# Attention scores and weighted sums in quarters of the TensorE array instead of halves

## The chip, the cores and the metric

The kernel runs on one core of a Trainium2 chip. The metric is the device time of one execution in microseconds (us). Before the change the median of three runs is 1355.07 us (1351.96 to 1355.53).

## The reference

One transformer layer: cross attention with 16 heads, then a three-layer feed-forward network with sign weights, both with a residual. Everything is float32. The change lies in the attention, so only that is shown:

```python
# x: (1, 2048, 256)   context: (1, 1601, 192)   16 heads of 64
x = layer_norm(x, g_norm)
q = x @ Wq                                   # 256 -> 1024
k, v = split(context @ Wkv)                  # 192 -> 2 x 1024
k = concatenate([null_k, k]); v = concatenate([null_v, v])    # 1602 keys per head
sim = einsum('bhid,bhjd->bhij', q * s, k * s)                 # s = 64 ** -0.25
sim = where(mask, sim, -big)
attn = softmax(sim)
out = einsum('bhij,bhjd->bhid', attn, v)
out = layer_norm(out.reshape(b, -1, 1024) @ Wout, g_out)
```

## The kernel before

**Units.** Two heads form a pair, and each head of a pair takes 64 partitions of the tensors that have the head dimension on partitions. There are 8 pairs (`NP`) and 4 blocks of 512 queries (`NB`), so 32 units (p, b), worked through in this order. The 1602 keys (`KEYS`) lie in 13 tiles (`KC`) of 128; the last has 66 (`KLAST`).

**A unit's score stage.** For each key tile k, `exps` issues the scores of both heads, keys on partitions and 512 queries along the free axis, into one of two PSUM tiles `sT` (L296). Each head is one float32 matmul with 64 rows of contraction and 128 columns of weights: the first head uses rows 0 to 63 of the array, the second rows 64 to 127, each writes its own PSUM bank. Keys are stored as differences: `keys_stepped` (GpSimd, L221) subtracts from each key tile the one two tiles back, so that the scores accumulate in the two PSUM tiles from k to k + 2. For k of 0 and 1 two more matmuls (L307, float32r, 64 × 128) add the negative row maximum. ScalarE then reads the tile, adds the mask as a bias per key and writes the exponentials `e` (L309). GpSimd adds the `e` of all key tiles into `acc` (L498, L500), from which the softmax denominator is made later.

Between the scores of one key tile and of the next, the unit issues work for the next unit's row maxima: `max_chunk`, two float32r matmuls of 64 rows by 128 columns over 400 keys (L259), one for each head, which VectorE reduces (L262). There are 16 of these chunks over 13 key tiles, two of them after key tiles 0, 4 and 8.

**A unit's sums stage.** `weighted` goes over the 13 key tiles once more and accumulates the weighted sums of values into `av` (L316): for each head one float32 matmul with 128 rows (keys) and 64 columns; the first head's result goes to partitions 0 to 63, the second's to 64 to 127, of the same PSUM bank. After the third key tile `divided` is called for the unit before: two float32 matmuls of 128 rows by 64 columns (L334) give the denominators, and VectorE takes the reciprocal and multiplies with `avs`. At the end ScalarE copies `av` from PSUM to `avs` (L542).

**Between the stages.** TensorE does projections for the next pair of heads (`project_k`, L207; `project_v`, L230), the output projection of the unit before (`project_out`, L324), a small transpose (L272) and the query projection (`project_q`, L196), all on the whole array.

**Order.** All of this is written out by hand in `tc.manual_schedule()`: instructions stand on each engine's queue in the order of the code. PSUM is split in two pools of two tiles of two banks each: `spare` (scores, `av`, output projection and some others) and `flex` (maxima, denominators and some others). Each further tile of a pool waits until its predecessor in the same buffer has been read.

Each float32 matmul shows as two matmuls, each with its weight load, in the trace; a float32r matmul shows as one.

Of the kernel before, what the change touches and what calls it, by code (L numbers as in the profile page):

```python
# [9 lines left out]
F32 = mybir.dt.float32  # L10
F32R = mybir.dt.float32r
U8 = mybir.dt.uint8
AF = mybir.ActivationFunctionType
ALU = mybir.AluOpType
# [6 lines left out]
KEYS = M + 1  # L21
CD = 192
HEADS, DH = 16, 64
# [3 lines left out]
NB = N // 512  # L27
KC = (KEYS + 127) // 128
KLAST = KEYS - 128 * (KC - 1)
CHUNKS = ((0, 402), (402, 400), (802, 400), (1202, 400))  # L30
EPS = 1e-5
MASKED = -3.0e38
# [3 lines left out]
def xattn_ffn(ctx, tc, x, ctxT, mask, g_norm, null_kv, wq, wkv, wout, g_out, k0, k1, k2, s0, s1, s2, out):  # L36
    nc = tc.nc
# [11 lines left out]
    def spare(name):  # L49
        return ps_s.tile([128, 2, 512], F32, tag="s", name=name)  # L50
# [92 lines left out]
    with ExitStack() as att:  # L143
        ap = att.enter_context(tc.tile_pool(name="att", bufs=1))
        pp = att.enter_context(tc.tile_pool(name="pair", bufs=2))
# [10 lines left out]
        maskb = ap.tile([128, KC], F32, name="maskb")  # L156
        ones_r = ap.tile([128, 128], F32R, name="ones_r")
# [23 lines left out]
        pairs, queries = {}, {}  # L181

        def open_pair(p):
            pairs[p] = (
                pp.tile([128, KEYS], F32, tag="kT", name=f"kT_{p}"),
                pp.tile([128, KC, 128], F32, tag="v", name=f"v_{p}"),
                pp.tile([128, KEYS], F32R, tag="kr", name=f"kr_{p}"),
            )

        def project_q(p, b, get=flex):  # L190

            qT = wp.tile([128, 512], F32, tag="qT", name=f"qT_{p}_{b}")
            qr = wp.tile([128, 512], F32R, tag="qr", name=f"qr_{p}_{b}", bufs=1)
            ps = get(f"psq_{p}_{b}")
            for c in range(2):
                nc.tensor.matmul(ps[:, 0, :], weights[p][0][:, c, :], xnT[:, b, c, :], start=c == 0, stop=c == 1)  # L196
            nc.scalar.mul(qr, ps[:, 0, :], DH**-0.5)  # L197
            nc.scalar.mul(qT, ps[:, 0, :], DH**-0.5)
            queries[p, b] = (qT, qr)

        def project_k(p, n, get=flex):
            kT, _, kr = pairs[p]
            start, w = CHUNKS[n]
            keys = ds(start, w)
# [11 lines left out]
        def keys_stepped(p):  # L216

            kT = pairs[p][0]
            for at in range(256 * ((KEYS - 1) // 256), 0, -256):
                w = min(256, KEYS - at)  # L220
                nc.gpsimd.tensor_tensor(kT[:, ds(at, w)], kT[:, ds(at, w)], kT[:, ds(at - 256, w)], ALU.subtract)  # L221

        def project_v(p, n, get=flex):
            v = pairs[p][1]
            tiles = range(4 * n, min(4 * n + 4, KC))
            rows = 128 if n < 3 else KLAST
            ps = get(f"psv_{p}_{n}")
# [23 lines left out]
        def max_chunk(p, b, n, get=flex):  # L251
            t, c = divmod(n, 4)
            if n == 0:
                maxima[p, b] = wp.tile([128, 4, 2, 4], F32, tag="mx", name=f"mx_{p}_{b}")
            start, w = CHUNKS[c]
            ps = get(f"max_{p}_{b}_{n}")
            for j in range(2):
                rows = ts(j, DH)
                nc.tensor.matmul(  # L259
                    ps[:, j, :w], queries[p, b][1][rows, ts(t, 128)], pairs[p][2][rows, ds(start, w)], start=True, stop=True  # L260
                )
            nc.vector.tensor_reduce(maxima[p, b][:, t, :, c], ps[:, :, :w], AX.X, ALU.max)  # L262
# [15 lines left out]
                ALU.mult,  # L278
            )

        def rows_of(k):
            return 128 if k < KC - 1 else KLAST

        def exps(p, b, k, sT):

            kT, qT, mT = pairs[p][0], queries[p, b][0], shifts[p, b]
            n = rows_of(k)
            ps = sT[k % 2]
            for j in range(2):
                rows = ts(j, DH)
                nc.tensor.matmul(  # L296
                    ps[:n, j, :],
                    kT[rows, ds(128 * k, n)],
                    qT[rows, :],
                    start=k < 2,  # L300
                    stop=k >= 2,
                    skip_group_check=k >= 2,
                )
            if k < 2:
                for j in range(2):
                    rows = ts(j, DH)
                    nc.tensor.matmul(ps[:n, j, :], ones_r[rows, :n], mT[rows, :], start=False, stop=True)  # L307
            e = ep.tile([128, 2, 512], F32, tag="e", name=f"e_{p}_{b}_{k}")
            nc.scalar.activation(e[:n], ps[:n], AF.Exp, bias=maskb[:n, k : k + 1])  # L309
            return e  # L310

        def weighted(p, k, e, av):
            v = pairs[p][1]
            n = rows_of(k)
            for j in range(2):
                nc.tensor.matmul(  # L316
                    av[ts(j, DH), 0, :], v[:n, k, ts(j, DH)], e[:n, j, :], start=k == 0, stop=k == KC - 1
                )

        def project_out(p, b, aoT):  # L320
# [55 lines left out]
        def load_x(b):  # L376
            nc.sync.dma_start(out=x_sb[:, ts(b, 4), :], in_=x[ts(b, 512), :].rearrange("(c p) d -> p c d", p=128))

        load_pair(0)
        for b in range(1, NB):  # L380
            load_x(b)
        for n, (at, w) in enumerate(CHUNKS):
            skip = 1 if n == 0 else 0
# [11 lines left out]
        for j in range(2):  # L395
# [6 lines left out]
        nc.gpsimd.dma_start(  # L402
            out=mcol_u8[:KLAST, KC - 1 : KC], in_=mask[ds(128 * (KC - 1) - 1, KLAST)].rearrange("(p o) -> p o", o=1)
        )
# [5 lines left out]
        for j, s in enumerate((s0, s1, s2)):  # L410
            nc.gpsimd.dma_start(out=s_sb[:, j : j + 1], in_=s.partition_broadcast(128))
        nc.gpsimd.memset(mcol, 0.0)
        nc.gpsimd.memset(maskb, 0.0)
        nc.gpsimd.memset(ones, 1.0)
        nc.gpsimd.memset(fan, 1.0)

        nc.scalar.activation(warm, eps_sb, AF.Sqrt)

        open_pair(0)
        xn = input_root(0)  # L420
        nc.vector.tensor_scalar(ones_r, ident, 0.0, 1.0, ALU.mult, ALU.add)
# [10 lines left out]
        for t in range(4):  # L432
            max_chunk(0, 0, 4 * t + 1, slot)
            if t == 1:
                project_k(0, 3, slot)
                keys_stepped(0)
# [6 lines left out]
        nc.vector.tensor_scalar(  # L443
            maskb[:KLAST, KC - 1 : KC], mcol_u8[:KLAST, KC - 1 : KC], -MASKED, MASKED, ALU.mult, ALU.add
        )
# [16 lines left out]
        with tc.manual_schedule():  # L462
            for u, (p, b) in enumerate(units):
                nxt = units[u + 1] if u + 1 < len(units) else None
                if b == 0 and p + 1 < NP:
                    load_pair(p + 1)
                    open_pair(p + 1)
# [16 lines left out]
                es, n = [], 0  # L484
                acc = lp.tile([128, 2, 512], F32, tag="acc", name=f"acc_{p}_{b}")
                for k in range(KC):
                    if k == 0:

                        odd = spare(f"sT_{p}_{b}_1")
                        sT = [spare(f"sT_{p}_{b}_0"), odd]  # L490
                    es.append(exps(p, b, k, sT))
                    for _ in range(2 if k in extra else 1):
                        if nxt is not None:
                            max_chunk(*nxt, n)
                            n += 1
                    m = rows_of(k)
                    if k == 1:
                        nc.gpsimd.tensor_tensor(acc, es[0], es[1], ALU.add)  # L498
                    elif k > 1:
                        nc.gpsimd.tensor_tensor(acc[:m], acc[:m], es[k][:m], ALU.add)  # L500
                if nxt is not None:
                    max_combined(*nxt)
                else:
# [13 lines left out]
                av = spare(f"av_{p}_{b}")  # L517
                for k in range(KC):
                    weighted(p, k, es[k], av)
                    if k == 2 and last is not None:  # L520
                        aoT = divided(*last, flex(f"den_{p}_{b}")[:, 0, :])
# [18 lines left out]
                    nc.vector.tensor_tensor(s_out, s_out, s_sb[:, 2:3], ALU.mult)  # L540
                avs = lp.tile([128, 512], F32, tag="avs", name=f"avs_{p}_{b}", bufs=1)
                nc.scalar.copy(avs, av[:, 0, :])  # L542

                if u < 2:
                    input_turned(u + 2)
                if p + 1 < NP:
                    for n in ahead[b][0]:
                        project_v(p + 1, n, spare if n % 2 else flex)
                    for n in ahead[b][1]:
                        project_k(p + 1, n, spare if n % 2 else flex)  # L550
                    if b == 2:
                        keys_stepped(p + 1)
# [143 lines left out]
```

## Time and profile before

| | |
|---|---|
| median of three runs | 1355.07 us |
| the profiled execution | 1355.55 us |
| its span, first to last instruction | 1353.7 us |
| granted TensorE clock | 0.992 |
| busy: TensorE, VectorE, ScalarE, GpSimd | 1329.3, 880.7, 607.7, 994.8 us |
| before the first unit's scores | 51.4 us |
| a unit's score stage | 16.5 us (the last unit 16.7) |
| a unit's sums stage | 12.2 us |
| between the stages | 3.7 to 8.6 us |
| the feed-forward network at the end | 191.6 us |

The stages are read from the timeline of TensorE: a score stage goes from the first matmul of L296 to the first of L316, a sums stage from there to the end of the last of L316. TensorE's matmuls overlap in the records, [...]so what one piece of work takes is read from end to end, not from its own recorded length.

### The profile page before, as it was taken

Reading aid. Unit: us, or ns where it says so; the run is one execution under the profiler, and the core shown is the slowest. Engines: PE = TensorE matmul, PEld = TensorE weight load, DVE = VectorE, ACT = ScalarE, POOL = GpSimd, SP = SyncE. Lnnn points to the kernel's source line nnn. Section 1 sums busy time; section 2 is a strip of 40 time slices with the busy share of each in tenths; the row PEclk is TensorE's granted clock in tenths of the full one; section 3 lists DMA queues with packets and bytes.
Section 4 is the critical chain, followed back from the end, with each engine's and each line's share of the span. In section 5 each row is a group of like instructions: output and inputs, shape, how many; then the busy total and the mean of one; then the engine's idle time right before and its main releaser. Section 6 shows DMA issues by size and latency. Waiting matters only on the chain.

```text
span 1353.7 us, 16255 instructions
## 1 busy us (share of the span) xinstructions
PE 1329.3 (98%) x6528; PEld 664.6 (49%) x6528; DVE 880.7 (65%) x957; ACT 607.7 (45%) x655; POOL 994.8 (73%) x492
## 2 busy tenths in 40 slices
PE   6999999999999999999999999999999999999998
PEld 3544444444444444444444444444444443688887
DVE  5677776676667756686767656767676884464431
ACT  1666454445444454444544454454445557421220
POOL 4377987798888987798779877987798999711100
PEclk9799999999999999999999999999999999999999
DMA  5000000000000000000000000000000010000000
GB/s 136 4 1 7 0 1 8 8 1 0 8 1 7 1 1 8 7 1 1 7 8 1 1 8 8 0 1 5 0 16 1 1 39 0 1 0 16 16 16 16
DMA packets 14940, 12.31 MB, mean 9 GB/s; under 512 B 2240, under 2 KB 14784, under 8 KB 14864
## 3 DMA queue, kind: packets, MB, share of 16 engines
q1 hardware_dynamic: 13552, 9.70, 2.5%
q10 hardware_dynamic: 832, 1.23, 0.3%
q8 instruction: 51, 0.84, 0.3%
q0 software_dynamic: 480, 0.34, 0.1%
q14 instruction: 25, 0.20, 0.1%
HBM read 9.17 MB, written 2.10 MB: 8 GB/s over the span
## 4 chain that ended last, share of the span: by engine, by line
PE 93%; DVE 3%; ACT 2%; DMA 1%; issue 0%; POOL 0%; SPq 0%; ACTq 0%
PE sT L296 28%; PE av L316 27%; PE ps L592 10%; PE max L259 8%; PE psq L196 4%; PE po L324 4%; PE psv L230 3%; PE psk L207 3%; PE ps L615 2%; PE den L334 2%; ACT e L309 1%; PE sT L307 1%; DVE mx L262 1%; DMA x_sb<-in_x 1%; PE xT L361 0%
## 5 line engine op out<-in xcount | busy, mean ns | idle before, releaser
L500 POOL TENSOR_TENSOR acc<-acc,e 128x1024 f32<-128x1024 f32 (+1 forms) x352 | 847.3, 2407 | 27.6
L262 DVE TENSOR_REDUCE mx<-max 128x2 f32<-128x800 f32 (+1 forms) x512 | 481.3, 988 | 70.9 <-PE max L259 61.2
L309 ACT ACTIVATE e<-sT,maskb 128x1024 f32<-128x1024 f32 (+1 forms) x416 | 460.0, 1115 | 64.0 <-PE sT L296 38.0
L296 PE MATMUL sT<-qT,kT 64*128 64x512 f32 (+1 forms) x1664 | 444.4, 612 | 1.6 <-ACT e L309 1.4
L316 PE MATMUL av<-e,v 128*64 128x512 f32 (+1 forms) x1664 | 369.5, 594 | 1.0
L259 PE MATMUL max<-kr,qr 64*128 64x400 f32 (+1 forms) x1024 | 285.7, 568 | 2.3 <-DVE mx L262 1.5
L316 PEld LDWEIGHTS av<-e,v 128*64 128x64 f32 (+1 forms) x1664 | 116.7, 137 | 239.0 <-issue 219.3
L259 PEld LDWEIGHTS max<-kr,qr 64*128 64x128 f32 x1024 | 97.3, 186 | 187.2 <-DVE mx L262 149.7
L296 PEld LDWEIGHTS sT<-qT,kT 64*128 64x128 f32 (+1 forms) x1664 | 135.3, 181 | 104.8 <-ACT e L309 81.5
L498 POOL TENSOR_TENSOR acc<-e,e 128x1024 f32<-128x1024 f32 x32 | 75.5, 2358 | 147.6 <-ACT e L309 147.6
L542 ACT COPY avs<-av 128x512 f32<-128x512 f32 x32 | 18.8, 587 | 327.0 <-PE av L316 327.0
L336 DVE RECIPROCAL aoT<-den 128x512 f32<-128x512 f32 x31 | 104.1, 3357 | 70.0 <-PE den L334 70.0
L197 ACT ACTIVATE qr<-psq 128x512 fp32r<-128x512 f32 x32 | 19.1, 597 | 139.1 <-PE psq L196 139.1
L592 PE MATMUL ps<-h0hi,w 128*128 128x512 f32 x256 | 79.5, 392 | 0.0
L592 PE MATMUL ps<-h0lo,w 128*128 128x512 f32 x256 | 78.9, 389 | 0.0
L211 DVE TENSOR_TENSOR kT<-psk,keep 128x400 f32<-128x400 f32 (+1 forms) x32 | 18.4, 574 | 90.0 <-PE psk L207 89.8
L119 POOL TENSOR_TENSOR y_sb<-y_sb,gout_sb 128x256 f32<-128x256 f32 x12 | 9.3, 776 | 90.1 <-DVE y_sb L86 90.1
L581 DVE SCALAR_TENSOR_TENSOR h1lo<-ps,h1hi 128x1024 fp32r<-128x1024 f32 x16 | 19.6, 1224 | 69.0 <-ACT h1hi L580 69.0
L196 PE MATMUL psq<-xnT,wq 128*128 128x512 f32 x128 | 62.2, 610 | 0.6 <-DVE kT L211 0.6
L324 PE MATMUL po<-wo,aoT 128*128 128x256 f32 x256 | 61.5, 383 | 0.0
L329 DVE TENSOR_TENSOR y_sb<-po,y_sb 128x1024 f32<-128x1024 f32 x28 | 34.2, 1220 | 40.0 <-PE po L324 39.8
L580 ACT ACTIVATE h1hi<-ps 128x1024 fp32r<-128x1024 f32 x16 | 16.4, 1027 | 94.6 <-PE ps L592 94.6
(125 smaller groups left out, 1054.8 us busy)
## 6 DMA issues: line engine op xcount, KB each, us to landing
x_sb<-in_x SPq DMA_DIRECT2D x4, 512.0 KB, 8.7
out_x<-o SPq DMA_DIRECT2D x8, 256.0 KB, 2.1
wkv<-in_wkv SPq DMA_DIRECT2D x16, 96.0 KB, 2.1
wq<-in_wq SPq DMA_DIRECT2D x8, 128.0 KB, 2.3
wo<-in_wout SPq DMA_DIRECT2D x8, 128.0 KB, 2.1
xnT<-in_k SPq DMA_DIRECT2D x1, 1024.0 KB, 5.9
ctx_sb<-in_ctxT ACTq DMA_DIRECT2D x3, 300.0 KB, 7.9
xnT<-in_k SPq DMA_DIRECT2D x1, 512.0 KB, 3.9
```

Of the source, the lines that this page charges most:

```text
L196: nc.tensor.matmul(ps[:, 0, :], weights[p][0][:, c, :], xnT[:, b, c, :], start=c == 0, stop=c == 1)
L207: nc.tensor.matmul(ps[:, 0, :w], weights[p][1][:, c, 0, :], ctx_sb[:, c, keys], start=c == 0, stop=c == 1)
L259: nc.tensor.matmul(ps[:, j, :w], queries[p, b][1][rows, ts(t, 128)], pairs[p][2][rows, ds(start, w)], start=True, stop=True)
L262: nc.vector.tensor_reduce(maxima[p, b][:, t, :, c], ps[:, :, :w], AX.X, ALU.max)
L296: nc.tensor.matmul(ps[:n, j, :], kT[rows, ds(128 * k, n)], qT[rows, :], start=k < 2, stop=k >= 2, skip_group_check=k >= 2,)
L309: nc.scalar.activation(e[:n], ps[:n], AF.Exp, bias=maskb[:n, k : k + 1])
L316: nc.tensor.matmul(av[ts(j, DH), 0, :], v[:n, k, ts(j, DH)], e[:n, j, :], start=k == 0, stop=k == KC - 1)
L324: nc.tensor.matmul(pv[:, t, :], aoT[:, ts(t, 128)], weights[p][2], start=True, stop=True)
L336: nc.vector.reciprocal(aoT, ps)
L498: nc.gpsimd.tensor_tensor(acc, es[0], es[1], ALU.add)
L500: nc.gpsimd.tensor_tensor(acc[:m], acc[:m], es[k][:m], ALU.add)
L592: nc.tensor.matmul(ps[:, f, :], w(c)[:, ts(2 * g + f, 128)], parts[part][:, c, :], start=i == 0, stop=i == len(steps) - 1,)
```

## The change

Scores: each head's matmul of 64 rows by 128 columns becomes two of 64 × 64, one for each half of the key tile, so that four matmuls per key tile use the four quarters of the array. Weighted sums: each head's matmul of 128 rows by 64 columns becomes two of 64 × 64, one for each half of the keys; the two key halves accumulate in two PSUM banks, and after the ScalarE copy of the first bank VectorE adds the second to it. The last key tile is filled up to 128 keys: the key and value tiles are cleared there by GpSimd, the mask bias is set so that the exponentials are zero, and every operation on it works on 128 rows. The maxima, the shift matmuls of L307 and the denominators stay as they were.

```diff
+KP = 128 * KC
...
         def open_pair(p):
             pairs[p] = (
-                pp.tile([128, KEYS], F32, tag="kT", name=f"kT_{p}"),
+                pp.tile([128, KP], F32, tag="kT", name=f"kT_{p}"),
                 pp.tile([128, KC, 128], F32, tag="v", name=f"v_{p}"),
                 pp.tile([128, KEYS], F32R, tag="kr", name=f"kr_{p}"),
             )
+            nc.gpsimd.memset(pairs[p][0][:, KEYS:], 0.0)
+            nc.gpsimd.memset(pairs[p][1][DH:, KC - 1, :], 0.0)
...
         def keys_stepped(p):
-            for at in range(256 * ((KEYS - 1) // 256), 0, -256):
-                w = min(256, KEYS - at)
+            for at in range(256 * ((KP - 1) // 256), 0, -256):
+                w = min(256, KP - at)
...
+        QUARTERS = ((0, 0), (0, 1), (1, 0), (1, 1))
...
-            for j in range(2):
+            for j, c in QUARTERS:
                 rows = ts(j, DH)
                 nc.tensor.matmul(
-                    ps[:n, j, :],
-                    kT[rows, ds(128 * k, n)],
+                    ps[ts(c, 64), j, :],
+                    kT[rows, ds(128 * k + 64 * c, 64)],
                     qT[rows, :],
...
-            nc.scalar.activation(e[:n], ps[:n], AF.Exp, bias=maskb[:n, k : k + 1])
+            nc.scalar.activation(e, ps, AF.Exp, bias=maskb[:, k : k + 1])
...
         def weighted(p, k, e, av):
-            for j in range(2):
+            for r, j in QUARTERS:
+                rows = ts(r, 64)
                 nc.tensor.matmul(
-                    av[ts(j, DH), 0, :], v[:n, k, ts(j, DH)], e[:n, j, :], start=k == 0, stop=k == KC - 1
+                    av[ts(j, DH), r, :], v[rows, k, ts(j, DH)], e[rows, j, :], start=k == 0, stop=k == KC - 1
                 )
...
-        nc.gpsimd.memset(maskb, 0.0)
+        nc.gpsimd.memset(maskb, MASKED)
...
-                        nc.gpsimd.tensor_tensor(acc[:m], acc[:m], es[k][:m], ALU.add)
+                        nc.gpsimd.tensor_tensor(acc, acc, es[k], ALU.add)
...
                 nc.scalar.copy(avs, av[:, 0, :])
+                nc.vector.tensor_tensor(avs, av[:, 1, :], avs, ALU.add)
```

## The prediction

> **What bounds the kernel now.** I read the page's busy times first, then its chain that ended last, then its costliest groups.
>
> ```profile
> PE 1329.3 (98%) x6528; PEld 664.6 (49%) x6528; DVE 880.7 (65%) x957; ACT 607.7 (45%) x655; POOL 994.8 (73%) x492
> ...
> PE 93%; DVE 3%; ACT 2%; DMA 1%; issue 0%; POOL 0%; SPq 0%; ACTq 0%
> PE sT L296 28%; PE av L316 27%; PE ps L592 10%; PE max L259 8%; PE psq L196 4%; PE po L324 4%; PE psv L230 3%; PE psk L207 3%; PE ps L615 2%; PE den L334 2%; ACT e L309 1%; PE sT L307 1%; DVE mx L262 1%; DMA x_sb<-in_x 1%; PE xT L361 0%
> ...
> L262 DVE TENSOR_REDUCE mx<-max 128x2 f32<-128x800 f32 (+1 forms) x512 | 481.3, 988 | 70.9 <-PE max L259 61.2
> L309 ACT ACTIVATE e<-sT,maskb 128x1024 f32<-128x1024 f32 (+1 forms) x416 | 460.0, 1115 | 64.0 <-PE sT L296 38.0
> ```
>
> TensorE owns the chain, and the two edited lines, L296 (scores) and L316 (weighted sums), are 55% of it. Since a busy TensorE is not TensorE at its peak, the next view is the timeline of its matmuls, around one passage into a score stage and one into the sums. Columns: start, length (us), line, tile, shape, count.
>
> ```profile
> 404.36 1.88 PE L196 MATMUL psq<-xnT,wq 128*128 128x512 f32 x4
> 406.17 1.13 PE L296 MATMUL sT<-qT,kT 64*128 64x512 f32 x4
> ...
> 408.85 0.41 PE L259 MATMUL max<-kr,qr 64*128 64x400 f32 x2
> 409.10 1.02 PE L296 MATMUL sT<-qT,kT 64*128 64x512 f32 x4
> ...
> 410.29 1.13 PE L296 MATMUL sT<-qT,kT 64*128 64x512 f32 x4
> 410.85 0.75 PE L259 MATMUL max<-kr,qr 64*128 64x402 f32 x2
> ...
> 421.88 0.75 PE L259 MATMUL max<-kr,qr 64*128 64x400 f32 x2
> 422.68 2.80 PE L316 MATMUL av<-e,v 128*64 128x512 f32 x12
> 425.30 1.03 PE L334 MATMUL den<-acc,ones 128*64 128x512 f32 x4
> 426.16 8.76 PE L316 MATMUL av<-e,v 128*64 128x512 f32 x40
> ```
>
> Ends are compared, as starts overlap. (1) One key tile of sums is two float32 matmuls, which run as four. The last 40 end 8.59 us after the four of the denominator (434.92 − 426.33): 0.215 us each, 0.86 us per key tile. (2) A key tile of scores costs the same: the four at 409.10 end 0.86 us after the maxima ahead of them (410.12 − 409.26). (3) A pair of maxima adds 0.18 us to the scores ahead of it (411.60 − 411.42).
>
> So a score stage needs 13 × 0.86 + 16 × 0.175 + 2 × 0.23 (the L307 pairs, by the same reading) = 14.4 us of TensorE. It lasts 16.5 us:
>
> ```profile
> 406.17:422.68 16.51, 16.47 (x90) 7.20 (x89) 14.17 (x17) 14.48 (x15) 11.97 (x6) 1.00 0.05 14
> 422.68:434.92 12.24, 12.24 (x57) 4.00 (x57) 7.40 (x4) 0.99 (x1) 11.93 (x5) 1.00 0.00 1
> ```
>
> (Window, length, then busy time of PE, PEld, DVE, ACT, POOL, with counts.) VectorE's 16 reductions at 0.988 us are 15.8 us and start 1.6 us into the stage, so VectorE sets its length, ScalarE is close (13 × 1.115 = 14.5 us) and TensorE has about 2 us of slack. The sums stage is TensorE alone: 13 × 0.86 + 0.86 + 0.2 = 12.2 us.
>
> **What the Trainium skill says.** "TensorEngine Tiling (Array Packing)", section Key Properties: changing the tiling mode, not just the tile, drains TensorE. The trace agrees and gives the price. From projection (whole array) to scores (two row halves) the four matmuls end 1.06 us after their predecessors (407.30 − 406.24) instead of 0.86: 0.20 us. From row-half maxima to column-half sums the first twelve take 2.85 us (425.48 − 422.63) against 12 × 0.215 = 2.58: 0.27 us, part of it perhaps a wait for the exponential. Between scores and maxima, both on row halves today, the price is nil by (2). The same page, section Restrictions and Gotchas, says different row tiles must write different banks; the edit's two banks obey that. "TensorE: Matmul & The Clock Gate", section The mechanism, has matmuls in strict program order. The trace disagrees: each float32 matmul runs twice in a row on its own tile, yet the four at 406.17 take 0.86 us of streaming and not the 1.29 that strict order would give, so matmuls of different tiles do pass each other. That matters for four tiles.
>
> **The change, part by part.**
>
> *Quartering, array work.* Two halves already fill the 128 × 128 array. Quarters make 8 runs per key tile where 4 were, each over the same 512 columns, four at a time instead of two: 2 rounds of 0.43 us before and after. Gain 0. The sums stage before already has two streams out of the same partitions, and the scores before already write two banks of the same partitions, so neither should slow the quarters. Issue: 16 weight loads and matmuls per 0.86 us are 54 ns each; twenty such pairs of L230, over 128 columns, take 2.49 us in the timeline from 398.85 on, about 0.2 us of it the first load and the last end, so 115 ns a pair where quarters need 107. At worst that is 8 × 8 = 64 ns per key tile, 27 us over the sums stages; in the score stages the switches leave issue time to catch up. I take 0.
>
> *Alternation, the cost.* Scores become 64 × 64 tiles while the maxima (L259) and shift matmuls (L307) stay 64 × 128 and are still issued after every key tile. So each key tile switches the mode twice. Per unit: 13 switches out of scores, 12 back in. Entry into the stage and exit to the sums switch mode already. At 0.195 us: 25 × 0.195 = 4.9 us. TensorE needs 14.4 + 4.9 = 19.3 us. That passes VectorE's 15.8 and ScalarE's 14.5, so the slack of 2 us is eaten first and TensorE sets the stage. With 0.2 us for entry and exit it is 19.5 us instead of 16.5: +3.0 us. What is queued behind a switch is everything, since TensorE issues in order; its readers (exp, reductions) merely idle. A score waits for the exponential two tiles back: 2 us apart in the new rhythm against 1.115 us plus handover, so no new wait there. 31 units have maxima: 31 × 3.0 = **+93 us**. The last has none: 4 switches in its first two key tiles, +0.4 us at most 0.8.
>
> *Denominator inside the sums.* L334 stays on 128 × 64 tiles amid quarters: two switches, 0.39 us, in 31 units: **+12 us**.
>
> *Added vector sum.* `avs` = bank 1 + `avs`, 128 × 512 from PSUM; nearest rows are L274 (0.68 us) and L211 (0.57 us). It starts after the ScalarE copy (0.59 us), about 1.4 us after the last sum. The space between stages hides it: there TensorE runs projections for 3.7 to 8.6 us and VectorE idles 3.8 us before its first eviction. The next but one PSUM tile of that pool is not asked for sooner than about 1.8 us after the sums. If the cover failed it would cost up to 0.7 us × 32 = 22 us. I take 0.
>
> *Padding and clearing.* 16 GpSimd clears of 62 and 128 columns (a 128 × 128 clear took 0.23 us), the last step of `keys_stepped` 128 wide instead of 66 (between 0.33 and 0.73 us), additions of 128 rows instead of 66 (2.41 against 2.40 us), full exponentials instead of 66 rows (1.115 against 1.111). GpSimd's 13 steps a unit, about 31 us, fit the shortest unit of 32.5 us and gain room as units lengthen. SP's loads are not moved. Cost 0.
>
> **Sum.** 93 + 12 + 0.4 = 105. The profiled execution took 1355.55 us (span 1353.7), half a microsecond above the median of 1355.07. So 1355.5 + 105 = **1460 us**.
>
> **Rivals.**
> - *Four streams don't run at once, only two.* Then every key tile costs 0.86 us more in both stages: 26 × 0.86 × 32 = +715 us, about 2175 us. For: no 64 × 64 tile appears in the trace. Against: the passing of matmuls shown above. 8%.
> - *The switch is free between quarters and row halves.* Then the score stage stays VectorE's at 16.5 us and only the denominator may cost: 1356 to 1368 us. Against: every change of tile shape that the trace has costs 0.2 us or more. 5%, three of it slower.
> - *Faster: a quarter's round is shorter than 0.43 us.* The place is the 52 rounds a unit in both stages. At a round of 0.43 − x the added 3.4 us per unit are paid back when 52x > 3.4, at x = 65 ns. At x = 115 ns the score stage is back at VectorE's limit and the sums are 2.6 us shorter, about 1355 − 32 × 2.6 = 1272 us. For: smaller weight loads (137 against 186 ns). Against: those are hidden already, as 0.43 us per round is the same at both load lengths. 5%.
> - That the quarters aren't issued as written can't be: the instruction order has four score matmuls per key tile.
>
> **Numbers.** The likeliest case has 82%. Its range comes from the price of a switch between 0.14 and 0.27 us (stage 18.2 to 21.4 us; 53 to 153 us, the denominator 9 to 17), plus at most 27 us for issue: 1410 to 1540 us. That leaves the other cases out. The smallest difference to be told from no change is about 0.3%, 4 us. Slower 92% (82 + 8, and part of the free switch), same 3%, faster 5%.
>
> **What would show it.** Right: a score stage of about 19.5 us with scores' and maxima's ends spread by 0.2 us at each alternation; VectorE and ScalarE waiting in it for TensorE; sums stage 12.6 us; about 1.44 us per key tile. Wrong: a key tile of sums at 1.7 us (no four streams) or clearly under 0.86 us; a score stage still at 16.5 us; TensorE waiting for the added vector sum.

## The result, and the profile after

The changed kernel takes 1448.21 us (median of four runs, 1445.68 to 1448.76) against 1353.71 us before, measured beside it: 1.0694 times as long, 95% interval 1.0672 to 1.0716. The forecast was 1460 us in 1410 to 1540. The profiled execution took 1448.76 us, its span is 1447.0 us, 93.3 us more than before.

The page of the changed kernel (its lines stand four lower or so: L299 is the scores, L320 the sums, L263 the maxima):

```profile
PE 1422.3 (98%) x9856; PEld 621.3 (43%) x9856; DVE 858.8 (59%) x989; ACT 611.0 (42%) x655; POOL 996.8 (69%) x508
...
L266 DVE TENSOR_REDUCE mx<-max 128x2 f32<-128x800 f32 (+1 forms) x512 | 490.4, 990 | 153.9 <-PE max L263 153.9
L312 ACT ACTIVATE e<-sT,maskb 128x1024 f32<-128x1024 f32 x416 | 463.4, 1114 | 141.5 <-PE sT L299 96.1
```

TensorE's 93 us more are all of the loss; no other engine works more than 3.3 us longer than before. VectorE's idle time ahead of the reductions has doubled (70.9 us to 153.9), and so has ScalarE's ahead of the exponentials (64.0 to 141.5): both now follow TensorE. The same view of TensorE's timeline as before, for the end of one score stage and the sums after it:

```profile
1025.02 1.09 PE L299 MATMUL sT<-qT,kT 64*64 64x512 f32 x8
1026.04 0.45 PE L263 MATMUL max<-kr,qr 64*128 64x400 f32 x2
1026.41 1.09 PE L299 MATMUL sT<-qT,kT 64*64 64x512 f32 x8
1027.43 0.46 PE L263 MATMUL max<-kr,qr 64*128 64x400 f32 x2
1027.82 2.81 PE L320 MATMUL av<-e,v 64*64 64x512 f32 x24
1030.55 1.08 PE L338 MATMUL den<-acc,ones 128*64 128x512 f32 x4
1031.56 8.81 PE L320 MATMUL av<-e,v 64*64 64x512 f32 x80
```

Read from end to end. From maxima to maxima (1026.49 to 1027.89) a key tile with one pair of maxima takes 1.40 us; 0.86 + 0.18 of it is work, 0.36 alternation. It divides so, by the medians over the whole trace: eight score matmuls end 1.02 us after the maxima ahead of them (here 1027.50 − 1026.49), 0.16 more than their work; the maxima end 0.38 after the scores (here 1027.89 − 1027.50), 0.20 more than theirs. The last 80 matmuls of the sums end 8.74 us after the denominators, where the same ten key tiles took 8.59 before: one re-entry of 0.16. The stages, in the windows' columns:

```profile
1008.62:1027.81 19.19, 19.19 (x141) 5.81 (x140) 14.45 (x16) 14.63 (x15) 14.17 (x6) 1.00 0.00 1
1027.81:1040.37 12.56, 12.56 (x111) 4.05 (x109) 5.23 (x4) 0.94 (x1) 12.17 (x6) 1.00 0.01 1
```

TensorE is busy in every moment of both. Summed over the 32 units, the score stages grew by 83.4 us (528.4 to 611.8) and the sums stages by 9.9 (390.8 to 400.7). That is all of the 93.3 us; the rest did not change.

One thing for the reading of what follows: the stretch ahead of the first scores took between 47.6 and 52.7 us in the profiles, whatever the edit. Differences of 3 us between medians are therefore read from the stages, which repeat to 0.03 us between units of a kind.

### The profile page after: what moved, and what is told of

It reads as the page before. It is cut to its first block, busy times and chain, and to the rows that moved or that the text cites. A ratio compares the mean times of both kernels' runs of the same rounds, so it can differ in the third digit from the quotient of the medians.

```text
span 1447.0 us, 22957 instructions
## 1 busy us (share of the span) xinstructions
PE 1422.3 (98%) x9856; PEld 621.3 (43%) x9856; DVE 858.8 (59%) x989; ACT 611.0 (42%) x655; POOL 996.8 (69%) x508
## 4 chain that ended last, share of the span: by engine, by line
PE 95%; DVE 2%; ACT 1%; DMA 1%; POOL 0%; issue 0%; SPq 0%; ACTq 0%
PE sT L299 29%; PE av L320 25%; PE max L263 11%; PE ps L596 9%; PE psq L200 4%; PE po L328 4%; PE psv L234 3%; PE psk L211 3%; PE den L338 2%; PE ps L619 2%; PE sT L310 2%; DMA x_sb<-in_x 1%; ACT e L312 0%; DVE mx L266 0%; PE xT L365 0%; PE mt L276 0%
## 5 line engine op out<-in xcount | busy, mean ns | idle before, releaser
L503 POOL TENSOR_TENSOR acc<-acc,e 128x1024 f32<-128x1024 f32 x352 | 845.6, 2402 | 27.6
L266 DVE TENSOR_REDUCE mx<-max 128x2 f32<-128x800 f32 (+1 forms) x512 | 490.4, 990 | 153.9 <-PE max L263 153.9
L312 ACT ACTIVATE e<-sT,maskb 128x1024 f32<-128x1024 f32 x416 | 463.4, 1114 | 141.5 <-PE sT L299 96.1
L299 PE MATMUL sT<-qT,kT 64*64 64x512 f32 x3328 | 453.0, 615 | 1.0 <-ACT e L312 1.0
L320 PE MATMUL av<-e,v 64*64 64x512 f32 x3328 | 371.6, 593 | 0.2 <-ACT e L312 0.2
L320 PEld LDWEIGHTS av<-e,v 64*64 64x64 f32 x3328 | 121.1, 133 | 227.1 <-issue 226.0
L263 PEld LDWEIGHTS max<-kr,qr 64*128 64x128 f32 x1024 | 93.5, 185 | 286.1 <-issue 152.1
L263 PE MATMUL max<-kr,qr 64*128 64x400 f32 (+1 forms) x1024 | 198.3, 416 | 3.9 <-DVE mx L266 3.1
L299 PEld LDWEIGHTS sT<-qT,kT 64*64 64x64 f32 x3328 | 86.4, 131 | 113.7 <-issue 86.2
L546 DVE TENSOR_TENSOR avs<-av,avs 128x512 f32<-128x512 f32 x32 | 22.1, 691 | 153.8 <-ACT avs L545 153.8
L211 PE MATMUL psk<-ctx_sb,wkv 96*128 96x400 f32 (+1 forms) x128 | 52.0, 540 | 6.0 <-DMA ctx_sb<-in_ctxT 4.9
```

The source lines that it names most:

```text
L211: nc.tensor.matmul(ps[:, 0, :w], weights[p][1][:, c, 0, :], ctx_sb[:, c, keys], start=c == 0, stop=c == 1)
L263: nc.tensor.matmul(ps[:, j, :w], queries[p, b][1][rows, ts(t, 128)], pairs[p][2][rows, ds(start, w)], start=True, stop=True)
L299: nc.tensor.matmul(ps[ts(c, 64), j, :], kT[rows, ds(128 * k + 64 * c, 64)], qT[rows, :], start=k < 2, stop=k >= 2, skip_group_check=k >= 2,)
L312: nc.scalar.activation(e, ps, AF.Exp, bias=maskb[:, k : k + 1])
L320: nc.tensor.matmul(av[ts(j, DH), r, :], v[rows, k, ts(j, DH)], e[rows, j, :], start=k == 0, stop=k == KC - 1)
L503: nc.gpsimd.tensor_tensor(acc, acc, es[k], ALU.add)
```

## The experiments

Theory A: a change of the tile shape costs TensorE time, the quarters themselves none. Theory B: small matmuls cost by their number. Theory C: float32 scores are slow in quarters.

**One half of the change at a time.** Each is the changed kernel with one loop set back to two halves:

```diff
e1_sums:    scores    for j, c in QUARTERS  ->  for j in range(2)   (64 x 128)
e2_scores:  sums      for r, j in QUARTERS  ->  for j in range(2)   (128 x 64), no vector sum
```

> Only the weighted sums are in quarters; scores are row halves (64 x 128) as before, the rest of the change stays. Theory A (each alternation of the tile shape costs a drain, 0.14 us into 64-column and 0.2 us into 128-column weights; the quarters themselves cost nothing): score stage 16.5 us as before, sums stage 12.56 us, so 1353.7 + 31 x 0.32 = about 1364 us. Theory B (the cost goes with the number of small matmuls, half of which are here): about 1400 us.

> Only the scores are in quarters; the sums are column halves in one bank as before, without the added vector sum. Theory A: score stage 19.2 us, sums stage 12.24 us, 1353.7 + 31 x 2.7 = about 1437 us. Theory B: about 1400 us.

e2 took 1436.41 us (1.062, 1.0602 to 1.0638): score stage 19.18, sums 12.24. The scores alone carry nearly all of the loss, although both halves bring equally many small matmuls: theory B is out. e1 took 1368.84 us (1.0116, 1.0101 to 1.0131), 5 us more than expected. Its sums stage is 12.56 us as expected; but every fourth score stage, that after `keys_stepped`, is 17.2 us where it was 16.55. The timeline of e1 there:

```profile
1013.02 2.82 DVE L216 SCALAR_TENSOR_TENSOR kr<-drop,nullk,kT 128x400 fp32r<-128x400 uint8 x1
1013.07 2.34 POOL L503 TENSOR_TENSOR acc<-acc,e 128x1024 f32<-128x1024 f32 x1
...
1018.05 0.68 DVE L278 TENSOR_TENSOR mT<-mt,fan 128x512 fp32r<-128x512 f32 x1
1018.79 0.50 PE L310 MATMUL sT<-mT,ones_r 64*128 64x512 f32 x2 [0.45 <-DVE mT L278]
```

The shift matmuls wait for VectorE, which has come late through its work between the stages; at this place before, they did not wait. The added vector sum is not what delays it: VectorE takes up the first piece of the new keys 1.58 us after the last sum, in e1 as in the kernel before. What is longer is the operation after it, L216 (L212 in the kernel before): 2.8 us in e1, 0.7 to 0.9 before and 0.7 in the changed kernel. In all three it ends some 0.44 us after the GpSimd addition beside it has ended (here 1015.84 against 1015.41), and in e1 that addition starts only after L216 does. So VectorE seems to be held by GpSimd there; no run tests this.

**The alternation turned round.** Scores and sums back in halves, the maxima and shift in quarters:

```diff
e3_flip (on e1 and e2 together):
-   for j in range(2): matmul(ps[:, j, :w], qr[rows, ts(t, 128)], ...)
+   for j, h in QUARTERS: matmul(ps[ts(h, 64), j, :w], qr[rows, ds(128 * t + 64 * h, 64)], ...)
+   kr, qr, ones_r, mT: bfloat16
e4_bf16 (on the changed kernel):
+   kr, qr, ones_r, mT: bfloat16
```

> Scores and sums as before in halves; instead the row maxima and the shift matmuls are in quarters, with their operands in bfloat16 (this type can be quartered; the maxima only shift the exponent). The same number of alternations, the other way round. Theory A: 13 x 0.14 + 12 x 0.2 = 4.2 us per score stage, stage about 19.1 us, 1353.7 + 31 x 2.6 = about 1435 us. Theory C (float32 scores are slow in quarters, for instance by weight loads or by two streams out of the same partitions): score stage 16.5 us, about 1354 us.

> The changed kernel with bfloat16 operands for the maxima and shift matmuls, which stay row halves: the control for the type alone. Theory A: the type plays no part, alternations as in the changed kernel, about 1448 us (within 3 us). If the type shortens the maxima or their weight loads: shorter by up to 16 x 31 x 0.05 = 25 us.

e3: 1415.34 us (1.046, 1.0444 to 1.0476), score stage 18.53. Scores in halves, and still two thirds of the loss: theory C does not explain that, the alternation does. (The other half of the argument is e9 below: scores in quarters, and no loss.) But e3 is 20 us under its expectation, and the control e4 shows why: 1401.71 us (1.036, 1.0344 to 1.0375), stage 17.78 instead of 19.19. The type was expected to play no part; it makes the switch cheaper. First e4, then e3, one alternation each:

```profile
432.17 1.09 PE L300 MATMUL sT<-qT,kT 64*64 64x512 f32 x8
433.19 0.34 PE L264 MATMUL max<-kr,qr 64*128 64x400 bf16 x2
433.46 1.09 PE L300 MATMUL sT<-qT,kT 64*64 64x512 f32 x8
```

```profile
432.94 1.13 PE L304 MATMUL sT<-qT,kT 64*128 64x512 f32 x4
434.00 0.36 PE L264 MATMUL max<-kr,qr 64*64 64x402 bf16 x4
434.30 1.13 PE L304 MATMUL sT<-qT,kT 64*128 64x512 f32 x4
```

In e4 the maxima end 0.28 us after the scores (here 433.53 − 433.26), not 0.38. The work of a pair is 0.17 in this type (0.18 before), so the switch into them is 0.11 instead of 0.20. Over 13 switches that is 1.2 to 1.3 us of the 1.41 gained per stage. The price follows what is loaded after the switch. The rows of the weight loads (mean ns of one), of the changed kernel, of e4 and of e3:

```profile
L263 PEld LDWEIGHTS max<-kr,qr 64*128 64x128 f32 x1024 | 93.5, 185 | 286.1 <-issue 152.1
...
L299 PEld LDWEIGHTS sT<-qT,kT 64*64 64x64 f32 x3328 | 86.4, 131 | 113.7 <-issue 86.2
```

```profile
L264 PEld LDWEIGHTS <-qr 64*128 64x128 bf16 x1024 | 51.3, 93 | 291.4 <-issue 283.9 <-ACT qr L202 1.5
```

```profile
L264 PEld LDWEIGHTS <-qr 64*64 64x64 bf16 x2048 | 58.0, 104 | 270.7 <-issue 265.8 <-ACT qr L202 1.5
```

| entered after a switch | weight load, mean, ns | first loads, ns | price of the switch, us |
|---|---|---|---|
| float32r, 64 × 128 (changed kernel) | 185 | 186 | 0.20 |
| float32, 64 × 128 (e3) | 184 | 190 | 0.20 |
| float32, 64 × 64 (changed kernel) | 131 | 149 | 0.16 |
| float32, 128 × 64 (changed kernel, denominators) | 134 | 139 | 0.15 |
| bfloat16, 64 × 64 (e3) | 104 | 113 | 0.12 |
| bfloat16, 64 × 128 (e4) | 93 | 96 | 0.11 |

The prices are medians over all alternations of a kind, from end to end, less the work as it runs without a switch. The third column goes from the start of the first to the end of the last of the two or four loads that fill the array; they start some ns apart. Each price is that time plus 10 to 16 ns. The trace also shows why. Here is the load of a pair of maxima, first in the changed kernel, then in the kernel before:

```profile
1026.03 0.19 PEld L263 LDWEIGHTS max<-kr,qr 64*128 64x128 f32 x2 [0.81 <-issue]
```

```profile
410.82 0.19 PEld L259 LDWEIGHTS max<-kr,qr 64*128 64x128 f32 x2 [0.24 <-DVE mx L262]
```

The scores ahead end at 1026.11 (1025.02 + 1.09) and at 411.42. In the changed kernel the load starts 0.07 us before that end (by the unrounded times), at every one of the 341 such switches, though it waits for nothing that the profile shows; before, it starts 0.59 us ahead in the median and runs beside the scores. So a change of shape lays the load open.

**Fewer alternations.** Maxima two at a time, after key tiles 1, 3, 5, 7, 9, 10, 11 and 12:

```diff
e8_grouped:
-   for _ in range(2 if k in extra else 1):
+   for _ in range({1: 2, 3: 2, 5: 2, 7: 2, 9: 2, 10: 2, 11: 2, 12: 2}.get(k, 0)):
```

> The changed kernel with fewer alternations: the maxima are issued two at a time after key tiles 1, 3, 5, 7, 9, 10, 11 and 12. Out of scores 9 times instead of 13, back 8 instead of 12. Theory A: 8 x 0.34 = 2.7 us less of drains per stage; TensorE would need 16.5 us; with waits for the reductions 16.8 to 17.8 us, 1375 to 1410 us. Theory B or C: same number of quarter matmuls, no gain, 1440 us or more.

1449.55 us (1.0711, 1.0694 to 1.0728), stage 19.33 us: no gain. The expectation has an arithmetic slip: four fewer switches each way are 4 × 0.36 = 1.4 us, not 2.7, and TensorE's need is then 17.8 us. The gain is spent on waits that the grouping brings, for the reductions above all (idle time in brackets):

```profile
486.22 0.45 PE L263 MATMUL max<-kr,qr 64*128 64x400 f32 x2
487.08 0.45 PE L263 MATMUL max<-kr,qr 64*128 64x400 f32 x2 [0.41 <-DVE mx L266]
...
490.92 0.45 PE L263 MATMUL max<-kr,qr 64*128 64x400 f32 x2 [0.20 <-DVE mx L266]
```

Read from end to end, the last three groups of maxima in this unit come 0.7, 0.2 and 0.5 us later than their work and switch take, and two groups of scores 0.1 each: 1.6 us, about the difference between 17.8 and the stage. Each remaining switch has its price unchanged (1.02 us into a key tile of scores). So e8 agrees with theory A, but its time alone would not show it.

**The added vector sum, and the denominators.**

```diff
e6_noadd:
-   nc.vector.tensor_tensor(avs, av[:, 1, :], avs, ALU.add)
e5_denq:
-   for j in range(2): matmul(ps[ts(j, DH), :], ones, acc[:, j, :])
+   for r, j in QUARTERS: matmul(ps[ts(j, DH), r, :], ones[rows, :], acc[rows, j, :])
+   nc.scalar.copy(aoT, ps[:, 0, :]); nc.vector.tensor_tensor(aoT, ps[:, 1, :], aoT, ALU.add)
```

> The changed kernel without the VectorE sum of the second bank, so the weighted sums lack the second half of each key tile. Theory A: hidden work, 1448 us, within 2 us. Rival (it delays the PSUM buffer of the sums or VectorE's next eviction): up to 0.7 x 32 = 22 us less.

> The changed kernel with the denominators in quarters too, row halves into two banks, brought together by one ScalarE copy and one VectorE sum ahead of the reciprocal. Theory A: the two alternations inside the sums stage go (12.56 to 12.24 us), 31 x 0.3 = 9 to 10 us less than the changed kernel, about 1438 us. Rival: the longer way to the reciprocal delays the output projection, no gain or a loss, 1448 us or more.

e6: 1445.67 us. All of its stages and the spaces between them are the changed kernel's (611.7, 400.7 and 191.5 us in sum against 611.8, 400.7 and 191.5); of the 3.3 us between the two profiled executions, 3.1 lie ahead of the first scores. In the changed kernel the sum is hidden. e5: 1449.12 us, no gain. Its sums stage is 12.25 us as theory A has it, 9.7 us less in all; but the space ahead of the last unit grew from 1.96 to 8.94 us, one early space from 8.08 to 9.91 and the end of the kernel from 191.7 to 195.9. There the ScalarE copy stands behind ScalarE's work for the normalisations. So the rival was right here, for three places.

**No alternation at all.** e7 is e5 with the maxima and shift of e3 on top: all of a unit's two stages in quarters. e9 is e7 with `nc.vector.tensor_copy` for the ScalarE copy. e11 is the kernel before with the four bfloat16 tiles and nothing else.

> Everything of a unit's two stages in quarters: scores, shift, maxima (bfloat16), denominators and sums, so that no alternation is left in either stage. Theory A: score stage back at VectorE's limit, and entry (0.14 for 0.2 us) and exit (no change of shape at all) cheaper: 16.2 us; sums 12.24 us or less; about 1353.7 - 31 x 0.25 = 1346 us. Theory B or C (quarters cost by themselves): well above 1354 us, up to the changed kernel's 1448.

> As e7_allq, but VectorE instead of ScalarE copies the first bank of the denominators. In e7 the stages were shorter as expected, and three passages between units were longer, where the ScalarE copy stood behind other ScalarE work. Theory A: those passages go back, the stages stay, 1353 - 9.6 = 1343 to 1345 us. Rival (the second bank itself costs, by the longer way to the reciprocal): no better than e7, 1359 us.

> The kernel before, with bfloat16 operands for the maxima and the shift only: control for e9. Theory A: no alternation inside its score stage, VectorE sets it, 1353 us within 3. If the type itself brings e9's gain: about 1344 us.

e7: 1359.21 us (1.0049, 1.0033 to 1.0066), score stage 16.12, sums 12.25, with e5's three late places. e9: 1346.06 us (0.994, 0.9925 to 0.9954), with the same stages; the two longer spaces between units are gone, and the end of the kernel is still 3.1 us longer than before (194.8 us). The clean comparison is with e4, which has the same type: with the alternations 1401.71 us and a score stage of 17.78, without them, all in quarters, 1346.06 and 16.12. A passage of e9 from scores to sums:

```profile
449.64 1.09 PE L304 MATMUL sT<-qT,kT 64*64 64x512 f32 x8
450.55 0.35 PE L264 MATMUL max<-kr,qr 64*64 64x400 bf16 x4
450.94 2.81 PE L325 MATMUL av<-e,v 64*64 64x512 f32 x24
453.57 1.04 PE L344 MATMUL den<-acc,ones 64*64 64x512 f32 x8
454.43 8.76 PE L325 MATMUL av<-e,v 64*64 64x512 f32 x80
```

But e11, in halves, takes 1341.98 us (0.9912, 0.9899 to 0.9925), with 16.14 and 12.24 us: the gain of e9 on the kernel before belongs to the type, as the second half of e11's expectation had it, and my likelier half was wrong. I had held VectorE for the only limit of the score stage before; yet its wait for the maxima falls from 61.2 us to 42.1 in e11, so it had not been. What in the type shortens that wait stays open. Halves or quarters in one shape throughout are equal to 0.02 us a stage, and 3.1 of the 4.1 us between e9 and e11 are that end of the kernel. e11 is the best version found, and the smallest edit.

**Maxima moved into the sums stage**, three per unit, after key tiles 5, 7 and 9, in e9's kernel (e10) and in e11's (e12). The step that combines the maxima moves behind the sums with them:

```diff
+   if k in {5, 7, 9} and nxt is not None: max_chunk(*nxt, n); n += 1      (in the loop over weighted)
```

> As e9, and three of the 16 maxima of a unit are issued in the sums stage, after key tiles 5, 7 and 9, where VectorE is idle; with everything in quarters that costs no alternation. Theory A: VectorE no longer sets the score stage; ScalarE does, 15.3 us instead of 16.1; sums 12.25 + 3 x 0.16 = 12.7 us; 31 x 0.3 = 10 us less than e9, about 1334 us. Rival (GpSimd's additions, about 31 us a unit, or VectorE's work after the sums hold it up): no gain on e9.

> As e11, and the same three maxima moved into the sums stage as in e10. Here sums are column halves and maxima row halves, so each moved pair costs two alternations. Theory A: score stage 15.4 us or so (-0.9 to -1.1), sums stage 12.24 + 3 x (0.16 + 0.105 + 0.145) = 13.5 us (+1.2): 31 x 0.2 = some 6 us more than e11, 1357 to 1365 us. Rival (alternation is free beside float32 sums): as e10 against e9, some 10 us less than e11.

Both missed. e10: 1403.67 us (1.0368, 1.0353 to 1.0384): score stage 15.74, sums stage 14.46 instead of 12.7. In e10 TensorE waits in the sums stage:

```profile
1038.96 0.36 PE L264 MATMUL max<-kr,qr 64*64 64x400 bf16 x4 [1.53 <-DVE mx L271]
```

The third pair waits for a PSUM buffer whose reduction stands behind the denominators' reciprocal on VectorE; over the kernel that is 47.3 us. The rival had VectorE's work after the sums; it was VectorE's work inside them. Two operations of 0.69 us that e9 and e10 have ahead of the reciprocal stand in that queue; in e12, which has neither, such waits are 5.3 us in the whole kernel. e12: 1377.28 us (1.0167, 1.015 to 1.0185), sums stage 13.52 us as expected (three pairs at 0.16 us and two switches each), but the score stage fell only to 15.87. There the loads of the scores wait for ScalarE for 193.6 us over the kernel (87.6 in e11): the limit that ScalarE sets is thus about 15.8 us and not 15.4. Where those 0.4 us come from stays open.

## Why the prediction was right

*Array work of the quarters, gain 0.* Right. A key tile of sums takes 0.86 us in the changed kernel (8.74 us for ten and a switch), scores likewise; the rival of two streams at a time (2175 us) is out, and so is a shorter round.

*Issue, 0.* Right: 80 small matmuls with their loads keep the pace of 0.86 us per key tile, one load-and-matmul pair in 107 ns.

*Alternation, +93 us.* Right in mechanism and place, 83.4 measured. The mis-sized term is the price of a switch: 0.195 us was taken for all 25. It holds for the 13 into 128-column weights (0.20); the 12 back into 64-column weights cost 0.16. 13 × 0.20 + 12 × 0.16 = 4.5 us instead of 4.9, and the entry from the projections is cheaper too (0.16): stage 19.19 instead of 19.5. The slack of 2 us was eaten first, as the sum had it: 4.5 us of switches lengthened the stage by 2.7.

*Denominator, +12 us.* 9.9 measured, the same term: both its switches enter 64-column weights, at 0.15 and 0.16 us.

*Vector sum and padding, 0.* Right for the changed kernel: e6 shows it for the sum, and outside the two stages no time was added. In e1, whose units are short, 4.3 us come back through VectorE's queue, but not through the added sum.

*The free switch* (1356 to 1368 us) is out by every run with an alternation.

Three details of the working do not hold, and none of them moves the forecast. The parts of the range add up to 1552 us at the upper end, not 1540. GpSimd adds 12 times a unit, not 13 (28.8 us). And that matmuls pass each other was read from the order of the calls: a trace shows when an instruction starts, not in which order it was issued. What the changed kernel's trace shows is that the first matmuls of all four quarters start within 0.02 us, and that the four are done at the pace of two halves.

The Trainium skill, "TensorE: Matmul & The Clock Gate", section LDWEIGHTS, says that a weight load's length goes with its columns: 64 columns fewer are 54 ns less here (185 to 131). By its formula 128 columns would take 107 ns, an estimate; the runs have 185, and the measurement counts. Its section "Weight-path perf modes — Fast Weight Load (FWL) and DoubleRow" has a faster load for 128 weights that are not float32; bfloat16's 93 ns against 185 (e4) agrees, and the 104 ns of only 64 bfloat16 columns (e3) fit it too. The 185 ns of float32r show no such gain. Had the weight loads been read beside the drain, the two prices of this change could have been told apart beforehand: the group rows before show 186 ns for 128 columns and 137 for 64.

## What to carry to other kernels

Ask of a tiled matmul not only whether its tiles fill the array, but what shape the next matmul has: two halves that fill it gained nothing as quarters here, and each change of shape lays the next weight load open (0.11 to 0.20 us here). In a loop that alternates between two kinds of matmul, count the changes and set them against the slack of the stage; bring all kinds to one shape, or leave them as they are. If a switch must stay, the entered side's weights set its price: it fell with fewer columns in float32 (0.20 to 0.16 us) and with a narrower type (0.20 to 0.11).

## What the runs showed that was not expected

A switch of shape costs no more than the weight loads that it exposes and 10 to 16 ns; six kinds of entry, from 96 to 190 ns of loads, fit. And a two-byte type for the row maxima, which only shift the exponent, shortened a stage thought to be VectorE's by 0.36 us of 16.5, 31 times over.
